# Cross attention with its largest scores subtracted from the scores themselves and its sums made on TensorE

## The chip, the cores and the metric

The kernel runs on one core of a Trainium2 chip. It is one launch. The metric is the device time of that launch in microseconds; what is given as the time is the median of several runs. One more execution was recorded by the hardware profiler, and all profile lines come from that one.

## The reference

The input is x of 2 x 1024 x 256 in f32, a context of 2 x 64 x 256 and a mask over the 64 context positions. Two blocks follow one another. Block 0 is self attention, cross attention on the normalized context, and a mixture of eight experts of which each row takes two. Block 1 is self attention, cross attention on the context as it is, with the mask, and one feed-forward layer. Each attention has 16 heads of 16 columns. What matters here is the cross attention:

```python
q = _heads(xn @ q_w.T)
k = _heads(codebook_embeds @ k_w.T)
v = _heads(codebook_embeds @ v_w.T)
attn = jnp.einsum('bhnd,bhmd->bhnm', q, k) * SCALE
bias = (1.0 - codebook_mask.astype(attn.dtype))[:, None, None, :] * -10000.0
attn = jax.nn.softmax(attn + bias, axis=-1)
ca = _merge(jnp.einsum('bhnm,bhmd->bhnd', attn, v)) @ ca_proj_w.T
x = x + ca
```

The softmax subtracts the largest score of each query and head before the exponential. Block 0 is the same with biases on queries, keys and values and without the mask.

## The kernel before

**Self attention as the backbone.** For each block a loop runs over 128 cells (64 for each of the two batch elements). A cell makes four score products whose maxima VectorE takes (`score`, kind "a", lines 753 and 760), LEAD = 10 cells ahead, and four transposed score products of which ScalarE takes the exponential (kind "b", lines 764 and 770). Every second cell multiplies the exponentials with V (line 815), ScalarE copies the result (line 827), and `helper()` adds it up (line 828). `helper()` is GpSimd as long as `maxima[0]` is true, that is, as long as cells have maxima to find, and VectorE afterwards. The order on TensorE, VectorE, ScalarE and SyncE is the order of the program; `tc.manual_schedule` names these four.

**The stream of other work.** All that isn't in the cells is a `Task` in a `Stream`: a generator that yields a positive cost for each step that it has issued, in planned microseconds, and a value of zero or less where it wants to wait, which moves its next step to a later cell (at least one). The loop takes steps from the stream at a pace of RATE (2.5 a cell in block 0, 1.1 in block 1) or as due dates demand. What is left after the last cell is issued by `Stream.rest`, by rank and planned time, among other tasks: expert slots in block 0 (lines 1544 and 1574), the feed-forward in block 1 (lines 1700 and 1712).

**Cross attention.** It is done in units of 512 queries, four for each block: a task for the layer norm, `weigh` and `share`. Once in each block `context_task` makes the keys (line 981, a mask row at line 989, small copies at lines 1000 and 1002) and values. The heads lie padded, 16 columns in strips of 32 partitions, so that the 16 heads fill four groups of 128 partitions. `weigh` makes the four groups of queries (line 1063, copied at line 1070), then scores only for their maxima (line 1082, reduced by VectorE at line 1089 into `spread_c`), transposes the maxima (line 1103, copied at line 1105) and subtracts them from a spare row of the queries (line 1108, `helper()`). Then it makes the scores again, transposed and with the maximum in the product (line 1124), takes the exponential (line 1133), multiplies with V and a column of ones (line 1141) and copies (line 1149). `send` writes the result and its sums to DRAM, `gather` reads it back without the padding, `invert` takes the reciprocal of the sums (line 492) and writes it, and `spread_out` reads it back, one row for each of a head's 16 partitions; `divide` multiplies (line 503). `share` issues the last of these and then the output projection (line 432, added to x at line 440).

Of the kernel before, what the change touches and what calls it, by code (L numbers as in the profile page):

```python
# [47 lines left out]
P = 128  # L49
# [5 lines left out]
HP = H * 32  # L55
# [15 lines left out]
NPAIR = 2 * 2 * B * 2 * 2  # L71
# [30 lines left out]
NCOL = 137  # L102

R_SEL = 0
NROW = 128


W_O, W_V, W_Q, W_K = 0, 512, 1024, 1536
NSELF = 2048
X_Q, NCROSS = 512, 1536  # L110

X_K, X_V, NCTX = 0, 1024, 1536
# [85 lines left out]
def two_blocks(  # L198
# [13 lines left out]
    rows_in: bass.AP,  # L212
# [24 lines left out]
    rows = const.tile([1, NROW], F32, name="rows")  # L237
# [24 lines left out]
    nc.sync.dma_start(out=rows, in_=rows_in)  # L262
    mask_i = const.tile([1, B * SK], I32, name="mask_i")
    mask_f = mask_i.bitcast(F32)
    nc.sync.dma_start(out=mask_i, in_=mask_in)
# [3 lines left out]
    nc.sync.dma_start(out=tri, in_=tri_in)  # L269

# [13 lines left out]
    spread_c = const.tile([P, 4, P], F32, name="spread_c")  # L284
# [7 lines left out]
    kbd = const.tile([P, 4, B, 4 * SK], F32, name="kbd")  # L292
    vbd = const.tile([P, B, H // 2, 64], F32, name="vbd")

    def other_constants():
        nc.gpsimd.memset(spread_c, 0.0)
        nc.gpsimd.memset(restart, 1.0)
        nc.gpsimd.memset(restart[:, :, 0:1], 0.0)
        nc.gpsimd.memset(kbd, 0.0)
        nc.gpsimd.memset(vbd, 0.0)  # L300
        for u in range(2):
            half = slice(SK * u, SK * (u + 1))
            nc.gpsimd.memset(
                vbd[half].rearrange("p b r c -> p (b r) c")[:, :, 32 * u + DH : 32 * u + 32], 1.0
            )
# [651 lines left out]
    def context_task(layer, w, c, pool):  # L957
# [20 lines left out]
        pk = pk.rearrange("p (g b k) -> p g b k", g=4, b=B)  # L978
        for g in range(4):
            for k in range(2):  # L980
                nc.tensor.matmul(
                    pk[:, g],
                    lhsT=w[:, X_K + k * HP + g * P : X_K + k * HP + (g + 1) * P],
                    rhs=kv[:, k, :].rearrange("p (b c) -> p b c", b=B)[:, :, :SK],
                    start=(k == 0),
                    stop=(k == 1 and layer == 0),
                )
            if layer == 1:
                nc.tensor.matmul(
                    pk[:, g], lhsT=rows[:, R_SEL : R_SEL + P],  # L990
                    rhs=mask_f.rearrange("p (b c) -> p b c", b=B), start=False, stop=True,
                )
            if g % 2 == 1:
                yield 1.8
        for g in range(4):
            for j in range(4):
                r = slice(32 * j, 32 * j + 32)
                dst, bias = kbd[r, g, :, SK * j : SK * (j + 1)], cols[r, C_K[att] + g : C_K[att] + g + 1]
                if layer == 1 and j % 2 == 1:
                    nc.vector.tensor_scalar(dst, pk[r, g], bias, None, ALU.add)  # L1000
                else:
                    nc.scalar.activation(dst, pk[r, g], AF.Identity, bias=bias)
            yield 0.3
# [13 lines left out]
        for u in range(2):  # L1017
            half = slice(SK * u, SK * (u + 1))
            for b in range(B):
                nc.scalar.copy(  # L1020
                    vbd[half, b, :, 32 * u : 32 * u + DH],
                    pv[half, b, :].rearrange("p (r v d) -> p r v d", v=2, d=DH)[:, :, u, :],
                )
# [3 lines left out]
    def cross_tasks(stream, layer, n, pool, first):  # L1027
# [8 lines left out]
        def norm():  # L1036
# [9 lines left out]
            weigh(layer, b, pool, w, name, held), 24.0,  # L1046
# [3 lines left out]
            share(pool, w, name, t0, held), 4.0, mark=("cross", n),  # L1050
# [3 lines left out]
    def weigh(layer, b, pool, w, name, held):  # L1054
# [4 lines left out]
        q = pool.tile([P, 4, 512], F32, tag="cq", name=f"q_{name}")  # L1059
        for g in range(4):  # L1060
            i, p = bank()
            for k in range(2):
                nc.tensor.matmul(  # L1063
                    p,
                    lhsT=w[:, X_Q + k * HP + g * P : X_Q + k * HP + (g + 1) * P],
# [8 lines left out]
            yield 1.72  # L1074

        for gp in range(2):
            for t in range(4):
                i, p = bank()
                p = p.rearrange("p (g n) -> p g n", g=2)
                for n in range(2):  # L1080
                    g = 2 * gp + n
                    nc.tensor.matmul(  # L1082
                        p[:, n, :],
                        lhsT=q[:, g, t * P : (t + 1) * P],
                        rhs=kbd[:, g, b, :],
                        start=True,
                        stop=True,
                    )
                nc.vector.tensor_reduce(
                    spread_c[:, t, :].rearrange("p (j r) -> p r j", r=32)[  # L1090
                        :, DH + 2 * gp : DH + 2 * gp + 2, :
                    ],
                    p.rearrange("p g (j k) -> p g j k", k=SK),
                    AX.X,
                    ALU.max,
                )
                free.append(i)
                if t % 2 == 1:
                    yield 2.0
        yield -1.5  # L1100
        i, mt = bank()
        for t in range(4):
            nc.tensor.transpose(mt[:, t * P : (t + 1) * P], spread_c[:, t, :], ident)
        mts = pool.tile([P, 512], F32, tag="osb", name=f"mts_{name}", bufs=2)
        nc.scalar.copy(mts, mt)
        free.append(i)
        for g in range(4):
            helper().tensor_tensor(q[:, g, :], q[:, g, :], mts, ALU.subtract)
        yield 1.0
        yield -5.2 if maxima[0] else -3.2  # L1110

        ot = q[:, 0:2, :]
        sums = [
            pool.tile([P, 32], F32, tag="sumc", name=f"sums_{name}{n}", bufs=2) for n in range(2)
        ]

        pairs = [next_heads() for _ in range(2)]

        def scores(g):
            pts = []  # L1120
            got = [bank() for _ in range(2)]
            for r in range(2):
                half = slice(64 * r, 64 * (r + 1))
                nc.tensor.matmul(  # L1124
                    got[r][1],
                    lhsT=kbd[half, g, b, P * r : P * (r + 1)],
                    rhs=q[half, g, :],
# [3 lines left out]
            for r in range(2):  # L1131
                pt = pool.tile([P, 512], F32, tag="p1", name=f"pt_{name}{g}{r}", bufs=4)
                nc.scalar.activation(pt, got[r][1], AF.Exp, scale=SCALE)
                free.append(got[r][0])
                pts.append(pt)
            return pts

        def product(g, pts):
            i, o = bank()
            for r in range(2):  # L1140
                nc.tensor.matmul(  # L1141
                    o[64 * r : 64 * (r + 1), :],
                    lhsT=vbd[:, b, 2 * g + r, :],
                    rhs=pts[r],
# [3 lines left out]
            osb = pool.tile([P, 512], F32, tag="osb", name=f"osb_{name}{g}", bufs=2)  # L1148
            nc.scalar.copy(osb, o)
            free.append(i)  # L1150
            return lambda: send(osb, pairs[g // 2], g % 2, sums[g // 2])

        todo, last = [], None
        for g in range(5):
            if g < 4:
                pts = scores(g)

            if todo:
                todo.pop(0)()
            if last is not None:  # L1160
                todo.append(product(*last))
            last = (g, pts)
            yield 2.1
        gather(pairs[0], ot[:, 0, :])
        todo.pop(0)()
        invert(pairs[0], sums[0])
        held.update(ot=ot, sums=sums, pairs=pairs)

    def share(pool, w, name, first, held):

        ot, sums, pairs = held["ot"], held["sums"], held["pairs"]
        by = [
            pool.tile([P, 512], F32, tag=tag, name=f"by_{name}{n}", bufs=bufs)
            for n, (tag, bufs) in enumerate((("by", 1), ("osb", 2)))
        ]
        yield -2.9
        spread_out(pairs[0], by[0])
        invert(pairs[1], sums[1])
        gather(pairs[1], ot[:, 1, :])
        yield -2.9  # L1180
        spread_out(pairs[1], by[1])
        divide(ot[:, 0, :], by[0])
        yield -3.8
        divide(ot[:, 1, :], by[1])
        if maxima[0]:
            yield -2.9
        for t0 in range(0, 4, 2):
            yield -1.4
            yield from project_task(ot, w, first + t0, t0, 2)
# [697 lines left out]
def _layout(inputs):  # L1887
# [8 lines left out]
    def heads_out(w):  # L1896

        t = np.zeros((2, P, H, 32), f32)
        t[..., :DH] = w.T.reshape(2, P, H, DH)
        return t.reshape(2, P, HP).transpose(1, 0, 2).reshape(P, 2 * HP)  # L1900

# [4 lines left out]
    def join(*parts):  # L1906
# [12 lines left out]
            join(plain(l0["ca_out_w"]), heads_out(c_in[0])),  # L1919
            join(plain(l1["ca_proj_w"]), heads_out(l1["q_w"])),  # L1920
# [4 lines left out]
            join(heads_out(c_in[1]), plain(c_in[2])),  # L1925
            join(heads_out(l1["k_w"]), plain(l1["v_w"])),
# [29 lines left out]
    def head_columns(bias, places):  # L1956

        t = np.zeros((4, 4, 32), f32)
        if bias is not None:
# [68 lines left out]
```

## Time and profile before

| what | value |
|---|---|
| time, median of 3 runs | 1692.17 us (1688.58 to 1693.54) |
| the profiled execution, its own time | 1687.93 us |
| its span, first to last instruction | 1685.9 us |
| mean granted TensorE clock | 0.982 |
| cells of block 0, then the rest of block 0 with expert slots | about 54 to 613 us, 613 to 1010 us |
| cells of block 1, then its rest | about 1010 to 1500 us, 1500 to 1686 us |

In a group's line stand the source line, the engine, what is written from what, the shapes and the count; behind the first bar the busy time in us and the mean of one in ns; behind the second bar the idle time of the engine just before, and what ended it. PE is TensorE's matmuls, PEld its weight loads, DVE VectorE, ACT ScalarE, POOL GpSimd, SP SyncE. A matmul in f32 shows as two records. The slices are 40 equal parts of the span with the busy share in tenths. The chain of waits is the work that ended last, followed back from the end: each piece with its start and length in us. In the timeline the brackets hold the idle time before an instruction and what ended it.

### The profile page before, as it was taken

The page shows a single profiled execution, that of the slowest core. Times are in us where ns is not written, and L with a number is a line of the kernel's source. Part 1 is how long each engine was busy: PE and PEld are TensorE (multiplying, and loading weights), DVE is VectorE, ACT ScalarE, POOL GpSimd, SP SyncE. Part 2 cuts the span into 40 slices and gives each one's busy share as a digit, 9 for nine tenths or more (in the row PEclk, how much of TensorE's full clock was granted, in tenths as well). Part 3 has the DMA queues.
Part 4 walks back from the last instruction along what each step waited for, and adds up shares of the span by engine and source line. Part 5 has one row for each costly group of instructions (what it writes and reads, how often), then busy time and mean ns, then how long its engine had stood idle before and what let it go on. Part 6 is the DMA issues. An engine that isn't in the chain of part 4 may idle for free.

```text
span 1685.9 us, 26108 instructions
## 1 busy us (share of the span) xinstructions
PE 1615.0 (96%) x9522; PEld 849.4 (50%) x9522; DVE 977.4 (58%) x2137; ACT 923.5 (55%) x1783; POOL 391.4 (23%) x479
## 2 busy tenths in 40 slices
PE   7989999999999987898999989999999999999998
PEld 3333344344434435687888854344344344335666
DVE  5658856587687635252211475976767677744420
ACT  2367866666665662333322316876766865774421
POOL 3124322232443302022111114421311331300000
PEclk8799999999999999999999999999999999999999
DMA  4333410210210144348556512100110112111100
GB/s 141 120 127 109 177 34 20 58 50 16 78 39 14 39 131 163 117 155 274 170 193 199 184 57 64 31 26 14 39 33 27 52 40 73 33 61 56 54 24 25
DMA packets 69739, 139.91 MB, mean 83 GB/s; under 512 B 17764, under 2 KB 31848, under 8 KB 69224
## 3 DMA queue, kind: packets, MB, share of 16 engines
q1 hardware_dynamic: 65768, 128.04, 23.6%
q0 software_dynamic: 3456, 9.51, 1.5%
q8 instruction: 77, 1.26, 0.3%
q10 hardware_dynamic: 384, 0.66, 0.2%
q14 instruction: 54, 0.44, 0.1%
HBM read 81.19 MB, written 48.07 MB: 77 GB/s over the span
## 4 chain that ended last, share of the span: by engine, by line
PE 84%; DVE 6%; DMA 5%; ACT 2%; issue 1%; SPq 1%; POOL 0%; DVEq 0%; ACTq 0%; POOLq 0%
PE banks L764 16%; PE banks L753 13%; PE banks L815 13%; PE banks L1544 7%; PE banks L1574 7%; PE banks L630 4%; PE banks L1063 3%; PE banks L1712 3%; PE banks L432 3%; PE banks L1082 3%; DVE mx_s L760 2%; PE banks L600 2%; PE banks L1700 2%; PE banks L1141 2%; PE banks L1124 1%; PE banks L364 1%
## 5 line engine op out<-in xcount | busy, mean ns | idle before, releaser
L760 DVE TENSOR_REDUCE mx_s<-banks 128x1 f32<-128x512 f32 x1024 | 635.3, 683 | 269.3 <-PE banks L753 266.5
L770 ACT ACTIVATE pt_s<-banks 128x512 f32<-128x512 f32 x1024 | 530.8, 607 | 164.7 <-PE banks L753 152.5
L753 PE MATMUL banks<-KS,QS 16*128 16x512 f32 x2048 | 523.1, 627 | 8.1 <-ACT pt_s L770 4.7
L764 PE MATMUL banks<-qb_s,KS 32*128 32x512 f32 x2048 | 501.2, 615 | 6.0 <-DVE qb_s L710 3.9
L828 POOL TENSOR_TENSOR acc_s<-acc_s,part_s 128x512 f32<-128x512 f32 x137 | 174.0, 1270 | 430.2 <-ACT part_s L827 428.9
L764 PEld LDWEIGHTS banks<-qb_s,KS 32*128 32x128 f32 x2048 | 171.9, 184 | 198.8 <-DVE mx_s L760 115.0
L815 PE MATMUL banks<-pt_s,v_s 128*20 128x512 f32 x2048 | 260.7, 601 | 0.2 <-ACT pt_s L770 0.2
L753 PEld LDWEIGHTS banks<-KS,QS 16*128 16x128 f32 x2048 | 194.8, 186 | 85.3 <-issue 41.4
L1550 ACT ACTIVATE h_s<-banks,w_slot 128x256 f32<-128x256 f32 x160 | 67.2, 471 | 178.1 <-PE banks L1544 101.3
L1544 PE MATMUL banks<-xsT,w_slot 128*128 128x256 f32 x640 | 149.5, 386 | 0.7 <-ACT xsT L371 0.7
L1574 PE MATMUL banks<-w_slot,h_s 128*128 128x256 f32 x640 | 144.9, 383 | 0.0
L815 PEld LDWEIGHTS banks<-pt_s,v_s 128*20 128x20 f32 x2048 | 43.5, 98 | 184.6 <-ACT pt_s L770 130.5
L1544 PEld LDWEIGHTS banks<-xsT,w_slot 128*128 128x128 f32 x640 | 120.9, 193 | 23.2 <-issue 3.0
L1574 PEld LDWEIGHTS banks<-w_slot,h_s 128*128 128x128 f32 x640 | 121.8, 192 | 20.2 <-DVE mx_s L760 1.5
L827 ACT COPY part_s<-banks 128x512 f32<-128x512 f32 x152 | 91.4, 601 | 58.1 <-PE banks L815 46.0
L1583 DVE SCALAR_TENSOR_TENSOR ys<-banks,gate,b 128x256 f32<-128x256 f32 x40 | 19.3, 483 | 142.7 <-PE banks L1574 141.5
L1589 POOL DMA_INDIRECT results<-ys,to x40 | 38.6, 966 | 257.0 <-DVE ys L1583 229.4
L630 PE MATMUL banks<-xT_s,w_att 128*128 128x512 f32 x128 | 68.0, 667 | 0.0
L1063 PE MATMUL banks<-xT_c,w_att 128*128 128x512 f32 x128 | 58.6, 602 | 1.3 <-ACT xT_c L371 1.3
L1082 PE MATMUL banks<-kbd,q_c 128*128 128x256 f32 x256 | 59.2, 383 | 0.0
L1712 PE MATMUL banks<-w_ff,h_f 128*128 128x256 f32 x256 | 57.3, 379 | 0.0
L1700 PE MATMUL banks<-hT_f,w_ff 128*128 128x512 f32 x128 | 56.2, 592 | 0.0
(265 smaller groups left out, 1398.6 us busy)
## 6 DMA issues: line engine op xcount, KB each, us to landing
w_slot<-in_ff_w_dram SPq DMA_DIRECT2D x40, 576.0 KB
w_slot<-in_ff_w_dram SPq DMA_DIRECT2D x40, 514.0 KB
sorted_rows<-fill SPq DMA_DIRECT2D x36, 520.0 KB
whole<-acc_s SPq DMA_DIRECT2D x32, 256.0 KB
whole<-osb_c SPq DMA_DIRECT2D x32, 256.0 KB
xs<-sorted_rows SPq DMA_DIRECT2D x20, 260.0 KB
ot_s<-whole SPq DMA_DIRECT2D x16, 256.0 KB
by_s<-turns SPq DMA_DIRECT2D x16, 256.0 KB
```

Of the source, the lines that this page charges most:

```text
L630: nc.tensor.matmul(p, lhsT=w[:, at + k * D + pair * P : at + k * D + (pair + 1) * P], rhs=xT[b][:, k, blk * 512 : (blk + 1) * 512], start= ...
L753: nc.tensor.matmul(sc, lhsT=QS[h % 4][r, qc * P : (qc + 1) * P], rhs=K[r, kh * 512 : (kh + 1) * 512], start=True, stop=True,)
L760: return i, lambda: nc.vector.tensor_reduce(mx[h][:, qc, j, kh : kh + 1], sc, AX.X, ALU.max)
L764: nc.tensor.matmul(sc, lhsT=K[r, n * P : (n + 1) * P], rhs=QB[h][r, :], start=True, stop=True)
L770: nc.scalar.activation(pt, sc, AF.Exp, scale=SCALE)
L815: nc.tensor.matmul(o[32 * j : 32 * j + VW, :], lhsT=V[b][:, cell % 8, 4 * g + j, :], rhs=exps.pop((cell, j)), start=(cell == cells[0]), st ...
L828: helper().tensor_tensor(acc[h], acc[h], part, ALU.add)
L1063: nc.tensor.matmul(p, lhsT=w[:, X_Q + k * HP + g * P : X_Q + k * HP + (g + 1) * P], rhs=xT[:, k, :], start=(k == 0), stop=(k == 1),)
L1082: nc.tensor.matmul(p[:, n, :], lhsT=q[:, g, t * P : (t + 1) * P], rhs=kbd[:, g, b, :], start=True, stop=True,)
L1544: nc.tensor.matmul(ph[:, n, :], lhsT=w[:, at : at + P], rhs=xT[:, k, :], start=(k == 0), stop=(k == 1),)
L1574: nc.tensor.matmul(py, lhsT=h1[:, f, h * P : (h + 1) * P], rhs=w[:, f * D : (f + 1) * D], start=(f == 0), stop=(f == 7),)
L1712: nc.tensor.matmul(py[:, n, :], lhsT=h1[:, f, t * P : (t + 1) * P], rhs=w2[:, f * D : (f + 1) * D], start=(f == 0), stop=(f == 7),)
```

## The change

Only cross attention, its context and the constants for it are changed.

- The padding goes. The 16 heads fill two groups of 128 partitions. Queries and keys take half of the matmuls. `kbd` holds for every strip of 32 partitions (two heads) two copies of the keys, each with the other head's rows set to zero by a scale column, so that one product over 32 partitions gives the scores of both heads.
- The scores are made once, queries in the partitions: for each group, four strips `r` and four blocks of 128 queries. In block 1 the mask is added by a product with one row, before each. VectorE takes the maxima. Then the maximum is subtracted from the scores: as long as `maxima[0]` is true ScalarE copies the scores to SBUF and GpSimd subtracts there; afterwards VectorE subtracts straight from PSUM.
- TensorE transposes the differences (`weights_turned`), ScalarE takes the exponential on the way out.
- `product` multiplies with V without a column of ones; the sums come from matmuls with a 0/1 table (`picks`), VectorE inverts them, `divided` spreads the inverses over the partitions with another part of the table, and VectorE multiplies. Nothing of cross attention goes through DRAM.
- The steps are issued in a list with their planned costs; while `maxima[0]` is true each step is followed by a wait for the next cell.

```diff
-        q = pool.tile([P, 4, 512], F32, tag="cq", name=f"q_{name}")
-        for g in range(4):
+        q = pool.tile([P, 2, 512], F32, tag="cq", name=f"q_{name}")
+        for g in range(2):
...
+        def scores(g, n):
+            got = [(r, *bank()) for r in (2 * n, 2 * n + 1)]
             for t in range(4):
+                for r, _, p in got if layer == 1 else ():
+                    at = slice(32 * r, 32 * r + 1)
                     nc.tensor.matmul(
+                        p[:, t * P : (t + 1) * P].rearrange("p (u k) -> p u k", k=SK),
+                        lhsT=ones[at, :],
+                        rhs=mask_f[at, b * SK : (b + 1) * SK].unsqueeze(1).to_broadcast([1, 2, SK]),
                         start=True,
+                        stop=False,
+                    )
+                for r, _, p in got:
+                    rows = slice(32 * r, 32 * r + 32)
+                    nc.tensor.matmul(
+                        p[:, t * P : (t + 1) * P],
+                        lhsT=q[rows, g, t * P : (t + 1) * P],
+                        rhs=kbd[rows, g, b].rearrange("p u k -> p (u k)"),
+                        start=(layer == 0),
                         stop=True,
                     )
+            for r, i, p in got:
+                p = p.rearrange("p (c k) -> p c k", k=SK)
+                mx = pool.tile([P, 8], F32, tag="mxc", name=f"mx_{name}{g}{r}", bufs=2)
+                sc = pool.tile([P, 512], F32, tag="sc", name=f"sc_{name}{g}{r}", bufs=4)
+                nc.vector.tensor_reduce(mx, p, AX.X, ALU.max)
+                sv, engine = sc.rearrange("p (c k) -> p c k", k=SK), nc.vector
+                if maxima[0]:
+                    nc.scalar.copy(sv, p)
+                    p, engine = sv, nc.gpsimd
+                engine.tensor_tensor(sv, p, mx.unsqueeze(2).to_broadcast(shape), ALU.subtract)
                 free.append(i)
+                less[g, r] = sc
+
+        def weights_turned(g, n):
+            for r in (2 * n, 2 * n + 1):
+                i, p = bank()
+                sc = less.pop((g, r))
+                for t in range(4):
+                    nc.tensor.transpose(
+                        p[:, t * P : (t + 1) * P], sc[:, t * P : (t + 1) * P], ident
+                    )
+                pt = pts[g, r] = pool.tile([P, 512], F32, tag="p1", name=f"pt_{name}{g}{r}", bufs=4)
+                nc.scalar.activation(pt, p, AF.Exp, scale=SCALE)
+                free.append(i)
...
+        def product(g):
+            i, o = bank()
+            for r in range(4):
                 nc.tensor.matmul(
+                    o[32 * r : 32 * (r + 1), :],
+                    lhsT=vbd[:, b, 4 * g + r, :],
+                    rhs=pts[g, r],
                     start=True,
                     stop=True,
                 )
+            j, s = bank()
+            for r in range(4):
+                for c in range(4):
+                    nc.tensor.matmul(
+                        s[32 * c : 32 * (c + 1), :P],
+                        lhsT=picks[:, O_SUM + 32 * r : O_SUM + 32 * (r + 1)],
+                        rhs=pts[g, r][:, c * P : (c + 1) * P],
+                        start=(r == 0),
+                        stop=(r == 3),
+                    )
+            nc.scalar.copy(q[:, g, :], o)
+            inv = inverse[g] = pool.tile([P, P], F32, tag="inv", name=f"inv_{name}{g}", bufs=2)
+            nc.vector.reciprocal(inv, s[:, :P])
+            free.extend((i, j))
+
+        def divided(g):
+            i, p = bank()
+            for c in range(4):
                 nc.tensor.matmul(
+                    p[:, c * P : (c + 1) * P],
+                    lhsT=picks[:, O_HEAD + c * P : O_HEAD + (c + 1) * P],
+                    rhs=inverse[g],
                     start=True,
                     stop=True,
                 )
+            nc.vector.tensor_tensor(q[:, g, :], q[:, g, :], p, ALU.mult)
             free.append(i)
+
+        cost = 1.9 if layer else 1.0
+        for step, args, us, wait in (
+            (scores, (0, 0), cost, None),
+            (scores, (0, 1), cost, -1.0),
+            (weights_turned, (0, 0), 1.3, None),
+            (scores, (1, 0), cost, None),
+            (weights_turned, (0, 1), 1.3, None),
+            (scores, (1, 1), cost, None),
+            (product, (0,), 1.75, None),
+            (weights_turned, (1, 0), 1.3, None),
+            (divided, (0,), 0.85, None),
+            (weights_turned, (1, 1), 1.3, -1.6),
+            (product, (1,), 1.75, None),
+        ):
+            step(*args)
+            yield us
+            if maxima[0]:
+                yield 0.0
+            elif wait:
+                yield wait
+
+    def share(w, name, first, held):
+        yield -1.5
+        held["divided"](1)
+        yield 0.85
+        yield -1.2
         for t0 in range(0, 4, 2):
+            yield from project_task(held["ot"], w, first + t0, t0, 2)
```

In the context the keys take two groups of two matmuls instead of four, the mask product there goes, and sixteen small copies become four:

```diff
-        for g in range(4):
-            for j in range(4):
...
+        for u in range(2):
+            for g in range(2):
+                bias = C_K[att] + 2 * u + g
+                nc.scalar.activation(
+                    kbd[:, g, :, u, :], pk[:, g], AF.Identity, bias=cols[:, bias : bias + 1],
+                    scale=cols[:, C_U + u : C_U + u + 1],
+                )
             yield 0.3
```

The cross attention weights have a third fewer columns (1024 instead of 1536), a table `picks` of 128 x 640 is loaded at the start, and the mask is loaded into all 128 partitions. The planned cost of `weigh` goes from 24 to 17 and that of `share` from 4 to 5.

## The prediction

> **What bounds the kernel now.** I read the page first, for the engine that is never free, then the groups of instructions kept apart by shape, for what cross attention costs each engine, then the chain of waits of the last stretch, where one unit of cross attention stands almost alone, and last the timeline, for the speed of short matmuls.
>
> ```profile
> PE 1615.0 (96%) x9522; PEld 849.4 (50%) x9522; DVE 977.4 (58%) x2137; ACT 923.5 (55%) x1783; POOL 391.4 (23%) x479
> PE   7989999999999987898999989999999999999998
> DVE  5658856587687635252211475976767677744420
> PE 84%; DVE 6%; DMA 5%; ACT 2%; issue 1%; SPq 1%; POOL 0%; DVEq 0%; ACTq 0%; POOLq 0%
> ```
>
> TensorE is busy in nearly every slice and makes 84% of the chain, VectorE 6%. TensorE work that goes away shortens the span, as long as nothing else becomes late.
>
> ```profile
> L1063 PE MATMUL banks<-xT_c,w_att 128*128 128x512 f32 x128 | 58.6, 602 | 1.3 <-ACT xT_c L371 1.3
> L1082 PE MATMUL banks<-kbd,q_c 128*128 128x256 f32 x256 | 59.2, 383 | 0.0
> L1124 PE MATMUL banks<-q_c,kbd 64*128 64x512 f32 x128 | 34.7, 628 | 0.0
> L1141 PE MATMUL banks<-pt_c,vbd 128*64 128x512 f32 x128 | 39.0, 616 | 2.0 <-ACT pt_c L1133 2.0
> L1108 POOL TENSOR_TENSOR q_c<-q_c,mts_c 128x512 f32<-128x512 f32 x20 | 25.3, 1297 | 6.8 <-ACT mts_c L1105 6.7
> L1108 DVE TENSOR_TENSOR q_c<-q_c,mts_c 128x512 f32<-128x512 f32 x12 | 7.5, 687 | 2.5 <-ACT mts_c L1105 2.5
> ```
>
> These are eight units (two blocks, four groups of 512 queries). An f32 matmul is two records, here called passes: 64 matmuls of L1063 give x128. L1108 tells where the helper is GpSimd: 20 of 32, so five units of eight run while maxima are being found.
>
> ```profile
> 1563.12 6.87 PE banks L1063 x16
> ...
> 1570.42 1.73 PE banks L1082 x8
> ...
> 1572.59 5.18 PE banks L1082 x24
> ...
> 1579.50 0.44 PE banks L1103 x4
> ...
> 1583.39 1.92 PE banks L1124 x8
> 1585.31 1.38 PE banks L1141 x4
> 1586.69 1.06 PE banks L1124 x4
> 1587.75 1.01 PE banks L1141 x4
> 1588.76 1.06 PE banks L1124 x4
> 1589.82 2.30 PE banks L1141 x7
> ```
>
> The last unit, in TensorE time: 6.87 + 6.91 + 0.44 + 4.04 + 4.69 = 22.95 us.
>
> ```profile
> 100.78 1.05 PE L981 MATMUL banks<-kvT,w_ctx 128*128 128x128 f32 x8
> ...
> 107.74 4.08 ACT L1002 ACTIVATE kbd<-banks,cols 32x128 f32<-32x128 f32 x11
> ...
> 709.53 2.93 PE L432 MATMUL banks<-w_att,q_c 128*128 128x256 f32 x6 [3.25 <-DVE q_c L503]
> ```
>
> Eight passes of 128 columns take 1.05 us with the last one's 0.27 us of latency: 0.11 us each. The other two are a stop of ScalarE and a stop of TensorE that the change touches.
>
> **The change, part by part.** Per unit, on TensorE:
> - Queries: two groups instead of four, half of 6.87: 3.44.
> - Scores: the old two products (L1082 for maxima, L1124 again transposed) become one: 32 matmuls of 128 columns, 64 passes, on two 32-row strips of the array at a time. L1124 shows two strips side by side: 8 passes in 1.92 where 8 x 0.43 = 3.44 would follow one another, a ratio of 0.56. So 64 x 0.11 x 0.56 = 3.9.
> - Block 1 adds as many mask matmuls: 3.9 again.
> - Transposes of the scores: 32, at L1103's 0.44 for four: 3.5.
> - Products with V: four 32-column strips, as L815 (16 passes of 512 in 1.84, ratio 0.27): 1.84.
> - Sums: 64 passes of 128 columns on four strips: 64 x 0.11 x 0.27 = 1.9.
> - Spreading the inverses: 16 passes: 1.8.
>
> Block 0 gives 3.44 + 3.9 + 3.5 + 1.84 + 1.9 + 1.8 = 16.4, block 1 20.3. Against 22.95: 6.55 and 2.65 saved, times four units each: **36.8 us**.
>
> No row shows passes of 128 columns on strips. [...] The trace's row is L981: weights are reloaded for every pass and it still runs at 0.11. [...] I take the row, which is this chip in f32 with the same reloading[...].
>
> Context, once per block: eight K matmuls fewer, 16 x 0.11 = 1.8 twice; block 1 also loses four mask matmuls (L989 holds the array 0.42 each): 1.7. ScalarE's 4.08 us of small kbd copies, behind which TensorE stands 4.71 us at 107.8 (its row at 112.49 names ACT pt_s), becomes four copies of L1002's 0.36: 1.4, so 2.6 of that stop goes. Together **7.9**.
>
> The trip through DRAM (send, gather, invert, spread_out) goes: 14 DMAs a unit, 112 on SP's queue at about 0.5 us of issue. SP isn't on the chain, so I give nothing for the issue. What counts is TensorE's idle time for the divided heads: 1.85 at 705.58, 3.25 at 709.53, 1.2 at 1550.4: **6.3**. Next in line there is the new sequence product, reciprocal, spread, multiply. Added transfers: the picks table (327 KB) and a mask broadcast to 128 rows, late on SP's start-up queue, which loses 256 KB of cross weights ahead of them: nothing.
>
> Other engines, per unit. While maxima are found: ScalarE gains eight copies of 0.6 and loses two query copies (0.69), one L1105 (0.61) and two L1149 (0.59): +1.6. GpSimd gets eight subtractions at L1108's 1.28 for four and two divisions: +2.6. VectorE keeps eight reductions, gains two reciprocals of 128 columns (0.13 for 2 columns at L417 and 0.345 for 32 at L492 give 7.2 ns a column: 1.03) and two multiplications of 0.69, loses two small reciprocals: +2.8. In the windows of the loops VectorE is busy 69 to 73 us of 100, ScalarE 61 to 74, GpSimd 33: there is cover. Without it each would be late at TensorE, 35 us over the five units.
>
> New waits. In the loop a transpose needs reduction, copy, then subtraction: matmuls 1.0, reductions queued ahead 2.5, its own 0.7, an acc addition ahead on GpSimd 1.27, two subtractions 2.55: 8.0 us. The step is put two cells later, and cells take 4.4 us in block 0 (128 from 54 to 613) and 3.8 in block 1 (128 from 1011 to 1497). So it arrives as it is needed. TensorE runs in order: when it waits, the next cell's scores wait, then VectorE and ScalarE. Twenty such steps at 0 to 1.5 us: 0 to 30; I take 5. In the three units after the maxima VectorE subtracts itself: eight times 1.38, 2.06 and 1.38 are 14.5 us a unit beside 16.4 or 20.3 of TensorE; set out step by step, the spread of group 0 waits for its reciprocal some 2 us and a transpose 1 to 2 in block 0, 1 in block 1: 6 in all. Together **-11**.
>
> Sum: 36.8 + 7.9 + 6.3 - 11 = 40. The profiled execution took 1687.9 (span 1685.9 and 2.0 around it): 1648. The median shown, 1692.2, lies 0.25% above it and would give 1652. I say 1650.
>
> **Rivals.**
> - Late hand-overs (0.17): the trip over ScalarE and GpSimd, or VectorE's 14.5 us, costs 25 to 30 instead of 11, nearer the upper bound. For it: four engines in sequence, GpSimd rows of 1.28. Against: two cells of distance. About 1670.
> - A larger gain (0.10): the freed SP queue and shorter tails also take the stops at 620.1 (6.4) and 650.4 (6.9), which hang on statistics and self attention's DMAs today. About 1633.
> - Slower (0.11): short passes on strips don't run side by side. Scores then cost 7.0 (+3.1), mask as much, sums 7.0 (+5.1): +8.2 a unit in block 0 and +11.3 in block 1, 78 in all: up to 1728, around 1712 if most is lost. It turns the sign when half of the overlap is missing (40 of 78): scores at a ratio of 0.78, sums at 0.64. For it: no row of the trace[...]. Against: L1124 and L815 share well at 512.
> - That the copying does nothing: it works only in the five units with maxima; the other three take the VectorE branch, already counted.
>
> **How the numbers follow.** The likeliest case, 1637 to 1663, has 0.62. A measurement here tells 0.3%, about 5 us, from no change. Range 1632 to 1684: it holds the likeliest and nearly all late hand-overs; left out are most of the slower case and the far end of the larger gain, below 0.2. Faster: 0.62 + 0.10 + most of 0.17 = 0.85; same 0.04; slower 0.11.
>
> **What would show it.** TensorE's busy time down by about 40. Score steps of 16 passes about 1.0 us long in block 0 and 2.0 in block 1; the sums' 32 passes about 1.0: near 1.7, 3.5 and 3.5 the slower case holds. Transposes with long waits on GpSimd or VectorE mean late hand-overs. No sums_c, turns or whole DMAs of cross attention. I am wrong if TensorE stays as busy in less work, or if the loops' VectorE share rises above 85%.

## The result and the profile after

The changed kernel takes 1678.4 us (median of five runs, 1676.9 to 1681.8) against 1690.9 for the kernel before in the same comparison: a ratio of 0.9929, with an interval of 0.9912 to 0.9946. It is 12.5 us faster where 40 were forecast: inside the stated range of 1632 to 1684, near its slow end, with less than a third of the gain. The profiled execution took 1676.9, its span is 1675.2.

The page of the changed kernel shows how little its busy times tell. This is the row with TensorE's:

```profile
PE 1614.0 (96%) x10682; PEld 881.3 (53%) x10682; DVE 995.2 (59%) x2148; ACT 913.5 (55%) x1768; POOL 401.5 (24%) x493
```

TensorE was busy for 1615.0 us before and is for 1614.0 now, although cross attention itself has less to do. The time must have gone to matmuls that were there before. The chain of the last unit (start, length, what) shows that the new matmuls themselves are cheap:

```profile
1551.92 0.42 PE banks L1072 x4
1552.34 0.22 PE banks L1081 x4
...
1573.27 0.87 PE banks L1131 x32
```

Four passes of scores take 0.22, that is 0.055 each where a single stream took 0.11: two strips do run side by side. The 32 passes of sums take 0.87, 0.027 each: four strips do. Counted from the start of one matmul to the start of the next over the whole trace, all lines of cross attention fall from 191.3 to 155.7 us, 35.6 less. Two groups of the changed kernel say who now waits for whom (line, busy time, mean in ns, and behind the second bar idle time and what ended it):

```profile
L1096 ACT COPY sc_c<-banks 128x512 f32<-128x512 f32 x40 | 23.4, 586 | 30.3 <-DVE mx_c L1092 30.1
L747 PEld LDWEIGHTS banks<-KS,QS 16*128 16x128 f32 x2048 | 199.5, 186 | 95.7 <-issue 37.6 <-ACT sc_c L1096 21.2 <-DVE mx_s L754 10.9
```

ScalarE's 40 copies stood idle for 30.1 us until VectorE's reduction was over, and the weight loads of the cells' next score products (L747, before the change L753) waited 21.2 us for these copies. The next table divides one profiled execution of each kernel into stretches, by the starts of TensorE's matmuls, with one experiment beside them. A loop runs from its first to its last transposed score product:

| stretch, us | before | changed | copy first (below) |
|---|---|---|---|
| loop of block 0 | 550.7 | 565.8 | 542.2 |
| of it in the cells' own three lines | 398.3 | 430.1 | 405.8 |
| rest of block 0 | 394.0 | 362.1 | 362.0 |
| loop of block 1 | 496.4 | 512.1 | 504.1 |
| of it in the cells' own three lines | 376.6 | 388.5 | 381.9 |
| from there to the last matmul | 179.1 | 169.7 | 169.6 |
| TensorE at half clock, whole span | 62 | 86 | 68 |

Outside the loops the change gains 41 us. Inside it loses 31. Not all of this is time won and lost: by the counts of passes, work has moved into the loops. Block 0's loop holds 96 passes of output projections where it held 80, block 1's 80 where it held 72, and block 1's loop holds the queries of three units and the scores of two and a half where it held two units. At the changed kernel's own times for these passes that is an estimated 13 us. The theory from this (A): ScalarE's copy and VectorE's reduction read the same PSUM bank one after the other, and this holds up the cells. Within it, A1 blames ScalarE's queue, where the exponentials of the next cell stand behind the waiting copy; A2 blames the bank, which TensorE gets back late. The rivals: the spacing of steps, the mixture's bookkeeping and the clock (B), GpSimd late (C), and VectorE simply having too much to do in the cells (D).

### The profile page after: what moved, and what is told of

Read it like the earlier page. It is cut to its first block, busy times and chain, and to the rows that moved or that the text cites. A ratio compares the mean times of both kernels' runs of the same rounds, so it can differ in the third digit from the quotient of the medians.

```text
span 1675.2 us, 28295 instructions
## 1 busy us (share of the span) xinstructions
PE 1614.0 (96%) x10682; PEld 881.3 (53%) x10682; DVE 995.2 (59%) x2148; ACT 913.5 (55%) x1768; POOL 401.5 (24%) x493
## 4 chain that ended last, share of the span: by engine, by line
PE 87%; DVE 8%; DMA 2%; issue 2%; ACT 1%; POOL 0%; SPq 0%; DVEq 0%; POOLq 0%; ACTq 0%
PE banks L758 16%; PE banks L747 15%; PE banks L809 14%; PE banks L1570 8%; PE banks L1540 8%; PE banks L624 4%; PE banks L1708 3%; PE banks L426 3%; PE banks L1696 3%; DVE mx_s L754 3%; PE banks L594 2%; PE banks L1051 2%; PE banks L1108 2%; PE banks L358 1%; PE banks L1081 1%
## 5 line engine op out<-in xcount | busy, mean ns | idle before, releaser
L747 PE MATMUL banks<-KS,QS 16*128 16x512 f32 x2048 | 543.9, 632 | 6.2 <-ACT sc_c L1096 2.9
L758 PE MATMUL banks<-qb_s,KS 32*128 32x512 f32 x2048 | 510.7, 619 | 6.0 <-DVE qb_s L704 3.7
L822 POOL TENSOR_TENSOR acc_s<-acc_s,part_s 128x512 f32<-128x512 f32 x141 | 179.3, 1272 | 454.8 <-ACT part_s L821 452.2
L809 PE MATMUL banks<-pt_s,v_s 128*20 128x512 f32 x2048 | 271.3, 618 | 1.3 <-DVE mx_s L754 1.0
L758 PEld LDWEIGHTS banks<-qb_s,KS 32*128 32x128 f32 x2048 | 177.4, 185 | 176.6 <-DVE mx_s L754 95.8
L747 PEld LDWEIGHTS banks<-KS,QS 16*128 16x128 f32 x2048 | 199.5, 186 | 95.7 <-issue 37.6
L821 ACT COPY part_s<-banks 128x512 f32<-128x512 f32 x157 | 94.8, 604 | 64.5 <-PE banks L809 54.4
L1699 ACT ACTIVATE h_f<-banks,w_ff 128x512 f32<-128x512 f32 x32 | 22.0, 688 | 81.1 <-PE banks L1696 81.1
L1092 DVE TENSOR_REDUCE mx_c<-banks 128x8 f32<-128x512 f32 x64 | 42.1, 682 | 32.8 <-PE banks L1081 27.9
L1098 POOL TENSOR_TENSOR sc_c<-sc_c,mx_c 128x512 f32<-128x512 f32 x40 | 40.9, 1045 | 76.6 <-ACT sc_c L1096 76.6
```

The source lines that it names most:

```text
L747: nc.tensor.matmul(sc, lhsT=QS[h % 4][r, qc * P : (qc + 1) * P], rhs=K[r, kh * 512 : (kh + 1) * 512], start=True, stop=True,)
L758: nc.tensor.matmul(sc, lhsT=K[r, n * P : (n + 1) * P], rhs=QB[h][r, :], start=True, stop=True)
L809: nc.tensor.matmul(o[32 * j : 32 * j + VW, :], lhsT=V[b][:, cell % 8, 4 * g + j, :], rhs=exps.pop((cell, j)), start=(cell == cells[0]), st ...
L821: nc.scalar.copy(part, o)
L822: helper().tensor_tensor(acc[h], acc[h], part, ALU.add)
```

## The experiments

Ratios are to the kernel before, run on the same chip in the same comparison (1690.6, 1692.8 and 1692.5 us in the three comparisons).

**The title's part undone.** VectorE subtracts in all eight units:

```diff
-                if maxima[0]:
-                    nc.scalar.copy(sv, p)
-                    p, engine = sv, nc.gpsimd
```

> The one part named in the change's title is undone: VectorE subtracts the largest score straight from PSUM in all eight units, with no copy by ScalarE and nothing for GpSimd. VectorE gains 40 subtractions of about 0.69 us (28 us), ScalarE loses 23 us, GpSimd 42 us. Theory A (the copy stands in ScalarE's queue behind VectorE's reduction of the same bank and holds the cells' exponentials, about 1 us for each of 40): the copying costs more than it saves, so this kernel is at least as fast as the changed one, 1655 to 1675. Rival B (what the cells lose comes from the waits between steps, from the placing of the mixture's bookkeeping and from the half clock, not from the copy): 1675 to 1690, since VectorE holds each bank 0.7 us longer. Rival C (late GpSimd): some 5 us faster, 1672.

Measured: 1716.6 us, ratio 1.0161 (1.0134 to 1.0188). All three missed: it is 38 us slower than the changed kernel. So copying is worth much, and A as I had put it, with the queue of ScalarE as the harm, can't be the whole. ScalarE has nothing of this in its queue here, and the cells wait longer.

**The copy first.** The same three instructions in another order. Since `p` then names the copy, VectorE also reads the scores from SBUF and no longer from the bank; the run after this one takes the two apart:

```diff
-                nc.vector.tensor_reduce(mx, p, AX.X, ALU.max)
                 sv, engine = sc.rearrange("p (c k) -> p c k", k=SK), nc.vector
                 if maxima[0]:
                     nc.scalar.copy(sv, p)
                     p, engine = sv, nc.gpsimd
+                nc.vector.tensor_reduce(mx, p, AX.X, ALU.max)
```

> The same work in another order: ScalarE copies the scores first, VectorE takes the maxima from the copy in SBUF, GpSimd subtracts as before. ScalarE no longer waits for VectorE, and the bank is freed by ScalarE alone. Theory A: most of the about 28 us of waits in the cells goes, and some of the half clock behind it: 1650 to 1665, and the copy's waits on the maxima (30.1 us in its group) fall to near nothing. Rival B: 1675 to 1680, no change that can be measured. Rival C: no change, since GpSimd gets its work as late as before.

Measured: 1646.7 us, ratio 0.9757 (0.9731 to 0.9782). That is 32 us less than the changed kernel, somewhat faster even than A's band; A holds, and as explanations of these 32 us B and C don't. TensorE is busy for 1584.2 us instead of 1614.0.

**The copy first, but both read the bank.** This tells A1 from A2:

```diff
-                nc.vector.tensor_reduce(mx, p, AX.X, ALU.max)
-                sv, engine = sc.rearrange("p (c k) -> p c k", k=SK), nc.vector
+                sv, engine, raw = sc.rearrange("p (c k) -> p c k", k=SK), nc.vector, p
                 if maxima[0]:
                     nc.scalar.copy(sv, p)
                     p, engine = sv, nc.gpsimd
+                nc.vector.tensor_reduce(mx, raw, AX.X, ALU.max)
```

> ScalarE copies the scores first, as in the version with the copy first, but VectorE then takes the maxima from the PSUM bank and not from the copy. ScalarE waits for nobody but TensorE, and yet the bank is held until the reduction is over. Theory A1 (what costs is ScalarE's queue: the exponentials of the next cell stand behind a copy that waits for VectorE): like the version with the copy first, 1645 to 1655. Theory A2 (what costs is how late TensorE gets the bank back, whoever reads last): like the changed kernel, 1670 to 1685. A mixture would lie between.

Measured: 1668.4 us, ratio 0.9862 (0.9835 to 0.9890), a shade below A2's band. Of the 32 us, about 10 come with the order alone, when ScalarE no longer waits, and about 22 only when the reduction no longer holds the bank. The timelines of one and the same kind of step, a score step in block 1 and the weight load that waits for its second bank, show it. First the changed kernel, then both reading with the copy first, then the copy first, then VectorE alone (start, length, engine, line, which differs by one or two between these kernels; in brackets the idle time before it and what ended it):

```profile
1243.46 0.39 PE L1081 MATMUL banks<-kbd,q_c 32*128 32x128 f32 x4
1243.95 1.29 DVE L1092 TENSOR_REDUCE mx_c<-banks 128x8 f32<-128x512 f32 x2 [1.37 <-PE banks L1081]
...
1244.67 1.19 ACT L1096 COPY sc_c<-banks 128x512 f32<-128x512 f32 x2 [2.10 <-DVE mx_c L1092]
...
1245.91 0.29 PEld L747 LDWEIGHTS banks<-KS,QS 16*128 16x128 f32 x2 [0.31 <-ACT sc_c L1096]
```

```profile
1235.70 0.39 PE L1081 MATMUL banks<-kbd,q_c 32*128 32x128 f32 x4
...
1236.12 1.07 ACT L1094 COPY sc_c<-banks 128x512 f32<-128x512 f32 x2 [1.31 <-PE banks L1081]
...
1236.80 1.29 DVE L1096 TENSOR_REDUCE mx_c<-banks 128x8 f32<-128x512 f32 x2 [1.99 <-ACT sc_c L1094]
...
1238.14 0.29 PEld L747 LDWEIGHTS banks<-KS,QS 16*128 16x128 f32 x2 [0.30 <-DVE mx_c L1096]
```

```profile
1217.30 0.39 PE L1081 MATMUL banks<-kbd,q_c 32*128 32x128 f32 x4
...
1217.72 1.07 ACT L1094 COPY sc_c<-banks 128x512 f32<-128x512 f32 x2 [1.31 <-PE banks L1081]
...
1218.40 1.28 DVE L1096 TENSOR_REDUCE mx_c<-sc_c 128x8 f32<-128x512 f32 x2 [1.99 <-ACT sc_c L1094]
...
1218.84 0.29 PEld L747 LDWEIGHTS banks<-KS,QS 16*128 16x128 f32 x2 [0.20 <-ACT sc_c L1094]
```

```profile
1268.34 0.39 PE L1081 MATMUL banks<-kbd,q_c 32*128 32x128 f32 x4
...
1270.81 0.69 DVE L1094 TENSOR_TENSOR sc_c<-banks,mx_c 128x512 f32<-128x512 f32 x1
...
1271.55 0.29 PEld L747 LDWEIGHTS banks<-KS,QS 16*128 16x128 f32 x2 [1.03 <-DVE sc_c L1094]
```

From the last score passes to the waiting weight load it is 2.45 us in the changed kernel, 2.44 with the copy first and both reading, 1.54 with the copy first, and 3.21 with VectorE alone. The order of the two readers makes no difference here (2.45 and 2.44); what counts is how many turns, one after another, stand before the weight load: three of some 0.65 us in the first two fences (the two engines overlap in one), two in the third, four in the last, where VectorE does all of them. In the third fence the reduction runs until 1219.68, and TensorE took the bank at 1218.84. The waits of that weight load in all, from the lists of waits (us, times, longest), rank in the same way; the changed kernel's 21.2 stood in its group above:

```profile
PEld banks L747 <- DVE mx_c L1096: 16.6, 37, 2.8
```

```profile
PEld banks L747 <- ACT sc_c L1094: 2.8, 14, 0.2
```

```profile
PEld banks L747 <- DVE sc_c L1094: 31.4, 36, 1.0
```

(both reading with the copy first; the copy first; VectorE alone.) For 17 of the 20 score steps in the loops I could also take the time of the cell right after, eight matmuls, from the last score pass to the first matmul after them, without other work between:

| mean us of the cell after a score step | block 0 (9) | block 1 (8) |
|---|---|---|
| changed | 4.03 | 3.32 |
| VectorE alone | 4.74 | 4.15 |
| copy first, both read the bank | 3.46 | 3.30 |
| copy first | 2.32 | 2.41 |
| copy alone, no maxima (below) | 2.36 | 2.41 |

From changed to copy first that is 9 x 1.71 + 8 x 0.91 = 22.7 us in 17 cells. In block 1 all of it is the bank. In block 0 the copy before the reduction gains 0.57 a cell while both still read the bank. That is the part that ScalarE's queue can explain: A1 is real, but smaller.

**Neither maxima nor subtraction in the loops.**

```diff
-                nc.vector.tensor_reduce(mx, p, AX.X, ALU.max)
...
                 if maxima[0]:
                     nc.scalar.copy(sv, p)
-                    p, engine = sv, nc.gpsimd
+                    free.append(i)
+                    less[g, r] = sc
+                    continue
+                nc.vector.tensor_reduce(mx, p, AX.X, ALU.max)
```

> In the five units of the loops the largest score is neither found nor subtracted: ScalarE's copy goes straight to the transposes (this leaves out the maxima and their subtraction there). VectorE loses 40 reductions (27 us), GpSimd 40 subtractions (42 us). Theory A with A2: the bank is free after 0.59 us and no more than in the version with the copy first, 1638 to 1647; what it gains beyond 1646.7 is what VectorE's reductions and GpSimd's lateness still cost, by the 5.9 us of weight loads that wait for GpSimd at most 8. If VectorE's load in the cells is itself the limit (rival D), 27 us less work gives much more: 1615 to 1630.

Measured: 1648.8 us, ratio 0.9729 (0.9700 to 0.9758); the interval overlaps that of the copy first. 40 reductions and 40 subtractions (25.7 and 40.9 us of two engines in the run with the copy first) cost nothing that can be measured, to some 5 us, once they no longer hold a bank. D falls, and C falls with it.

**More buffers for the maxima.** `bufs=2` becomes `bufs=8` for the tile `mxc` in the changed kernel.

> Eight buffers instead of two for the tile of the largest scores of cross attention, so that VectorE's reduction never waits for GpSimd's subtraction two steps before. Theory A: the chain GpSimd, VectorE, ScalarE, TensorE is cut once or twice (at 413.5 us it was 1.76 + 2.86 us and then seven us at half clock): 3 to 6 us faster, 1672 to 1675. Rival C: this is the main path, 10 to 20 us, 1658 to 1668. Rival B: nothing, 1678.

Measured: 1671.7 us, ratio 0.9897 (0.9874 to 0.9921). 6.7 us by the medians, just beyond what A gave and far from C's main path; the interval still touches that of the changed kernel. This is the chain that it cuts, in the changed kernel:

```profile
413.50 0.69 DVE L1092 TENSOR_REDUCE mx_c<-banks 128x8 f32<-128x512 f32 x1 [1.76 <-POOL sc_c L1098]
414.22 0.59 ACT L1096 COPY sc_c<-banks 128x512 f32<-128x512 f32 x1 [3.77 <-DVE mx_c L1092]
...
414.86 3.06 PE L747 MATMUL banks<-KS,QS 16*128 16x512 f32 x4 [2.86 <-ACT sc_c L1096]
```

The third reduction needs a buffer that GpSimd's subtraction frees; ScalarE waits for the reduction, TensorE for ScalarE. The reduction ends at 414.19 and the copy starts at 414.22. Behind the stop the granted clock is at half from 415.3 to 422.1.

**The bookkeeping in five pieces.** In the task that numbers the expert slots in the loop of block 0, a `yield -0.1` (wait for the next cell) after the tile counts and after each of three parts of `Places`.

> The bookkeeping that numbers the expert slots in the middle of block 0's loop, some 30 small VectorE operations at one place, is cut into five pieces with a cell between two of them. Theory B: the stop of 7.2 us at 541.7 us and the 13.6 us at half clock behind it go, less what stood there before the change: 6 to 12 us faster, 1666 to 1672. Theory A: at most 2 us, since the stop is only moved: 1676 to 1678.

Measured: 1671.7 us, ratio 0.9896 (0.9875 to 0.9917). 6.7 us by the medians, inside B's band; this interval touches that of the changed kernel too. Windows over the bookkeeping in the changed kernel, in this run, where its pieces are spread over 18 us, and in the kernel before (length, TensorE, weight loads, VectorE, ScalarE, GpSimd busy, then the clock):

```profile
541.00:549.00 8.00, 0.81 (x5) 0.18 (x2) 7.42 (x28) 0.90 (x2) 6.33 (x6) 0.75 0.24 84
```

```profile
548.00:566.00 18.00, 18.00 (x112) 7.16 (x110) 15.29 (x41) 9.86 (x18) 6.21 (x7) 0.83 0.05 16
```

```profile
551.00:559.00 8.00, 8.00 (x43) 2.89 (x42) 6.37 (x32) 4.58 (x8) 5.05 (x5) 1.00 0.19 70
```

TensorE does 0.81 us of work in the 8 us of the first and is busy throughout in the other two. B has a true part, but a small one beside the 32 us of the bank.

**The same pieces in the kernel before.**

> The kernel before the change, with the bookkeeping in five pieces. There it cost a stop of 4.0 us at 501.6 us and 7 us at half clock. If the cost belongs to the bookkeeping and not to the change: 4 to 7 us faster than before, about 1685. If the change made it dear: 0 to 2 us, about 1689.

Measured: 1690.5 us, ratio 0.9992 (0.9976 to 1.0008): nothing. The expectation looked at the wrong place: the stop at 501.6 us is not the bookkeeping's. VectorE is there at four scalings of rows for the experts (line 1226, 5.09 us). The bookkeeping of the kernel before lies at 551.6 to 555.6 us, beside a TensorE that is busy throughout, so there was nothing to gain. In the changed kernel it takes 7.4 us where it took 4.0, and nearly all of the difference is two small operations. This is one, before and changed:

```profile
551.95 0.17 DVE L1386 COPY end<-begin 128x8 f32<-128x8 f32 x1
```

```profile
541.25 1.96 DVE L1382 COPY end<-begin 128x8 f32<-128x8 f32 x1
```

The other, a subtraction of 15 columns, takes 1.81 us where it took 0.17. In the changed kernel each ends 0.04 us after an addition of GpSimd; in the kernel before no addition of GpSimd falls into this stretch. So what made the bookkeeping dear is, by these rows, where it fell; no run moved GpSimd's additions alone.

**All three together.** Copy first, eight buffers, five pieces.

> The copy first, eight buffers for the maxima and the bookkeeping in five pieces, all together. If the three are separate: 1646.7 less up to 6.7 for the buffers and 6.7 for the pieces, 1634 to 1640. By theory A the buffers are worth nothing once ScalarE and the bank don't wait for the reduction: 1640 to 1644.

Measured: 1640.8 us, ratio 0.9695 (0.9671 to 0.9719), 3% below the kernel before and over 2% below the changed one. Beyond the copy first it is another 6 us, at the lower end of what A allows; the two small corrections don't add up to their 13.4.

**The copy also after the loops.** `if maxima[0]` becomes `if True` around the copy.

> The version with all three corrections (1640.8), and ScalarE's copy with GpSimd's subtraction also in the three units after the loops, where VectorE subtracts straight from PSUM and a bank is held for a reduction and a subtraction, 1.37 us. If the late bank costs there as it does in the loops: 3 to 6 us faster, 1635 to 1638. If those stretches have other work between the steps, so that the bank is not needed: no change, 1639 to 1642. If GpSimd's 1.04 us for each subtraction comes late at the transposes: 2 to 6 us slower, 1643 to 1647.

Measured: 1638.9 us, ratio 0.9686 (0.9660 to 0.9712). It can't be told from 1640.8. Either the late bank costs little where expert slots or the feed-forward stand between the steps, or GpSimd's longer subtraction (in the changed kernel 1.045 us where VectorE's takes 0.691) takes back what the bank gains; this run doesn't part the two.

**Steps without a wait for the next cell.**

```diff
-            if maxima[0]:
-                yield 0.0
-            elif wait:
+            if wait:
                 yield wait
```

> The version with all three corrections (1640.8), without the wait for the next cell after each step of a unit in the loops; two fixed waits stay. Theory A (a score step disturbs only through the bank, which is now soon free): steps may stand closer, 1636 to 1645. Rival B (the spacing of the steps matters, since two score steps behind one another give VectorE four reductions and transposes come before GpSimd is done): 1650 to 1665.

Measured: 1646.6 us, ratio 0.9738 (0.9707 to 0.9768). That lies between the two bands. The intervals touch; if anything it is 6 us slower, so the waits between the steps are not what cost the time. Of B that leaves the bookkeeping and the clock; wider spacing was not tried.

## Why the prediction fell short, point by point

- **TensorE's own work: right.** 36.8 us forecast, 35.6 measured. Per unit the queries took 3.6 (3.44 forecast), block 1's mask 3.8 (3.9), the products with V 1.75 (1.84), the sums 2.0 (1.9). Only the transposes were dearer, 4.6 instead of 3.5. The difference is right in part by luck, since both sides were taken too low: the old work took 191.3 where the prediction's 22.95 a unit give 183.6, and the new 155.7 where it gives 146.8.
- **Short passes: the row was right.** The prediction took 0.11 us for a pass of 128 columns from the row of L981; with 35.6 of 36.8 us measured there is no room for a much dearer one. The slower rival needed scores at a ratio of 0.78; 0.055 against 0.11 is 0.50.
- **Context and DRAM trip: right in sum.** The two lines of the keys fell by 4.2 where 7.9 were given to the context, stop included. Part of that was a wrong count: four matmuls fewer for the keys of a block, 8 passes, and not eight matmuls, so 1.8 us for both blocks and not twice 1.8. The line of the output projection fell by 15.2 where 6.3 were given. The stops that the larger-gain rival named, at 620.1 (6.4) and 650.4 (6.9), are gone: in the rest of block 0 the stops over 1 us fall from 23.3 to 7.1 us in all. Outside the loops the change brought 41 us where the prediction's terms give about 16; about 13 of the 41 are the work that moved into the loops, and the two stops were another 13.3.
- **New waits: the step that failed.** The prediction put 5 us into the loops. It followed each score tile forwards, reduction, copy, subtraction, transpose, and asked when the transpose could start. That part was right: the transposes' weight loads wait 4.0 us for GpSimd's subtractions. It never asked when the bank goes back to TensorE, so it put that wait at nothing, and its sum of 8.0 us has no term for the copy that stands behind the reduction. The loops were to give 24 us (three units of 6.55, two of 2.65, half of the context, less 5) and lost 31. Of these 55 us, 32 are shown to be the two readers' turns at the bank, about 22 by the bank itself and 10 by ScalarE's queue; the two small corrections take another 6 beside it. Even with all three corrections the loops gain only 4 us on the kernel before. Of the remaining 17 or so, about 13 are no loss but the work that moved in. The last few are not settled, and single executions can't settle them: block 1's loop took 496.4 us in the kernel before and 502.9 in the run with the pieces in that kernel, which has the same block 1. Of the rivals, late hand-overs (about 1670) came nearest in number, but not by the path that it named.
- **Two readers of one bank took turns.** In the changed kernel it is 30.1 us of idle time before the copies, and in the timeline 0.03 us from the end of a reduction to the start of its copy; with the copy first and both reading the bank, the reductions wait 15.4 us for the copies. The kernel before has a case that I should have weighed, the small copies of block 1's keys, which both engines make from one bank:

```profile
826.85 0.34 ACT L1002 ACTIVATE kbd<-banks,cols 32x128 f32<-32x128 f32 x1
827.22 0.34 DVE L1000 TENSOR_SCALAR kbd<-banks,cols 32x128 f32<-32x128 f32 x1 [7.16 <-ACT kbd L1002]
...
827.60 0.36 ACT L1002 ACTIVATE kbd<-banks,cols 32x128 f32<-32x128 f32 x1 [0.41 <-DVE kbd L1000]
...
827.99 0.36 DVE L1000 TENSOR_SCALAR kbd<-banks,cols 32x128 f32<-32x128 f32 x1 [0.43 <-ACT kbd L1002]
```

Each of the four starts 0.03 or 0.04 us after the one before it ends; in all VectorE stood idle for 12.8 us until such copies of ScalarE were over. They write one tile as well as they read one bank, so these rows don't show which of the two sets the turns. Taken for the bank, they give each score step a reduction and a copy in sequence on each bank, and the price could have been read from the rows of before: 0.68 and 0.6. Letting both engines read one bank at once was not tried.
- **The sign of error that it named came true**: TensorE was as busy in less work. With the copy first the kernel takes 1646.7, against 1650 forecast, but that is in part luck: by the table the loops then gain 1 us where 24 were forecast, and 41 come from outside the loops where 16 were. The work that moved accounts for some 13 on each side; the rest, some 10 too little inside and 12 too much outside, happens to cancel.
- **VectorE's load**: 70% of the loops' windows in block 0 and 73% in block 1, below the 85% at which I would have been wrong. A share of busy time shows nothing of a bank that is held.

## What to carry to other kernels

When two engines read one PSUM bank, count their turns: here the weight load that needed the bank next came 1.54, 2.45 and 3.21 us after the score passes for two, three and four turns, though VectorE was busy for only 59% of the changed kernel's span and ScalarE for 55%. Let one engine copy the bank out first and give the other the copy in SBUF (32 us here); work that no longer holds a bank can be free, as 67 us on two engines were here within what could be measured. In a sum of an edit's costs, follow each buffer back to its writer as well as each value forward to its reader. And before two stretches are compared, count what work stands in each.

## What the runs showed of the hardware that I had not expected

**The granted clock was lower with VectorE alone.** Its mean over the span was 0.973 to 0.983 in the runs of the kernel before, 0.967 to 0.974 in those of the changed kernel and 0.951 to 0.958 in those with VectorE alone. Windows of block 0's loop, of before, changed and VectorE alone (the column after the five busy times is the granted clock):

```profile
54.00:620.00 566.00, 552.94 (x3633) 231.08 (x3631) 390.29 (x752) 378.40 (x730) 172.00 (x223) 0.98 0.21 70
```

```profile
54.00:620.00 566.00, 548.56 (x3908) 240.29 (x3906) 396.38 (x756) 368.41 (x707) 177.90 (x232) 0.96 0.18 58
```

```profile
54.00:620.00 566.00, 547.82 (x3702) 235.37 (x3706) 404.86 (x770) 341.89 (x654) 153.11 (x208) 0.92 0.18 58
```

TensorE stands idle for 13.1, 17.4 and 18.2 us of these 566, at a clock of 0.98, 0.96 and 0.92; with the copy first it is 23.1 us at 0.97, so the idle time alone doesn't tell the clock. Summed over the whole span, TensorE was at half clock for 62, 86 and 161 us, and for 68 with the copy first. VectorE alone lost 38 us, where its 0.76 us more at the bank (3.21 less 2.45) explain 15 in 20 steps. Of the 75 us more at half clock 61 lie in the loops; by an estimate from the granted clock of 0.50 they cost up to half of themselves, and so they can hold the rest. That the waits of one cell after another brought the clock down is read from the order of things in the trace and was not tested apart.

**A small VectorE operation took 3.21 us and ended as GpSimd's did.** In the run with the pieces, a copy of 8 columns in SBUF took 3.21 us, where the next copy of 8 columns takes 0.16:

```profile
548.77 3.21 DVE L1382 COPY end<-begin 128x8 f32<-128x8 f32 x1
...
550.67 1.27 POOL L418 TENSOR_TENSOR x_sb<-x_sb,bias_out 128x512 f32<-128x512 f32 x1
```

It ends at 551.98, 0.04 after the second of two additions of GpSimd (the first starts at 549.46), as the two operations of the changed kernel end 0.04 after one. That it waited for GpSimd is read from these ends alone and was not tested apart; which of the two came first the row doesn't show well, since the copy starts 0.69 us before the first addition.
